# Two graph-attention layers: the fourth bank of each burst of scores is the held bank of the output products

## The chip, the cores and the metric

The kernel runs on one core of one Trainium2 chip. The metric is the device time of one execution in microseconds (us); of several executions the median is taken. Everything is computed in fp32.

## What is computed

64 examples of 256 nodes with 512 features pass through two layers with a residual each. The first is a graph attention with one head of 256 features, the second an attention with 8 heads of 64. Both are masked by one 256 x 256 adjacency. Cut to what matters here, the second layer is:

```
h = relu(layernorm(x))
q, k, v = heads(h @ Wq.T + bq), heads(h @ Wk.T + bk), heads(h @ Wv.T + bv)   # 8 heads of 64
scores = einsum('bhqd,bhkd->bhqk', q, k) / 8
scores = where(adj == 0, -inf, scores)
out = einsum('bhqk,bhkd->bhqd', softmax(scores), v)
x = x + out @ Wo.T + bo
```

## The kernel before

**Tiling and stages.** The examples go in 32 groups (g) of two (b = 0 and 1). All matmuls of the main part go through one helper (L136 and L137, so they all stand under L137), which ties each to the one before it: TensorE's order is exactly the program's order. On the other engines many operations are tied to the one before in the same way (`not_sooner`, L123, whose operations stand under L35), and a scheduler that works from its own estimate of times places the rest. The projections and the output products are done as seven half-size products each, whose operands are sums (`sums`, `o_sums`), which is why two or three accumulators are open for several products.

**The order of the work.** For each g and b a string (L1174 to L1184) is worked off letter by letter. Before it comes `weigh` (L1036) of the example before: 64 matmuls `pr` (values times probabilities, tiles of 128 x 32 of the array) into two banks, which VectorE multiplies by the reciprocal row sums `r` into `oT`. Then come the letters: S is a burst of scores (L933), m masks a pair of heads, u is one of the 21 projection products of the next group (`pq`, `pk`, `pv`), s a piece of the first layer of the group after that (`ph`, `po`, with its softmax numerator `e`), n a piece of its layer norm, f a step of the row sums (`fold`, L982: SyncE writes the probabilities to DRAM and reads them back as `parts`, POOL adds, VectorE transposes and sums them into `compact`), and o one of the seven output products of the example before (`outputs`, L1080, `py`). For b = 0, S is followed by u in the first places of TensorE's work, for b = 1 by u and s; in the last group it is followed by o. VectorE's addition of an output product into x is `x<-py,x`.

**A burst of scores.** Eight heads come as four pairs. The two heads of a pair use the upper and the lower 64 rows of the array, so their matmuls run side by side, and each head has one bank. ACT takes one exponential per head (`p<-sc`), in the order of the heads. In the traces each fp32 matmul stands as two records, so a burst has 32.

**Banks.** PSUM tiles come from four tags of one pool. `turn` has five banks that rotate; the scheduler gives a new tile the bank that it takes to come free first. Three more tags have one bank each:

```
    def mm(name):
        return psum.tile([P, 512], F32, tag="turn", name=name, bufs=5)

    def held_bank(n, name):
        return psum.tile([P, 512], F32, tag=f"held{n}", name=name, bufs=1)
```

Banks 0 and 1 of these hold the two long accumulators of the projections (L903, L914). Bank 2 holds the first accumulator of the output products (L1095), which takes four of the seven products with an addition into x after each; the other two accumulators of `outputs` (L1099, L1106), the two banks of `pr` (L1060) and all scores come from `turn`. Between the last addition of one example's `outputs` and the first product of the next one's, in which time `weigh` and the burst lie, bank 2 is empty.

Of the kernel before, what the change touches and what calls it, by code (L numbers as in the profile page):

```python
# [57 lines left out]
def bounded(  # L58
# [31 lines left out]
    NT = N // P  # L90
# [18 lines left out]
# [6 lines that stand above are left out]
    def after(instruction, name):  # L115

        tc.add_manual_dep(
            instruction.ins, name,
            mybir.DependencyInfo(mybir.DependencyClass.NoSync, mybir.DependencyReason.DATA),
            reason="the engine's order",  # L120
        )
# [14 lines left out]
    def matmul(*args, **kwargs):  # L136
        in_order(nc.tensor.matmul(*args, **kwargs))  # L137
# [795 lines left out]
    def scores(g, b):  # L933

        (q, q_tag), (k, k_tag) = (qkv[name, g, b] for name in "qk")
        name = f"{g}_{b}"
        p = att.tile([P, NQ * QH, NT, N], F32, tag="p", name=f"p_{name}", bufs=1)
        for i in range(HP):  # L940
            sc = [mm(f"sc_{name}_{2 * i + j}").rearrange("p (k n) -> p k n", k=NT) for j in range(2)]
            for kb in range(NT):
                for j in range(2):
                    rows = slice(j * DH, (j + 1) * DH)
                    matmul(
                        sc[j][:, kb, :], k[rows, i, kb * P : (kb + 1) * P], q[rows, i, :],
                        start=True, stop=True,
                    )
            pair = p[:, 2 * i : 2 * i + 2]
            for j in range(2):  # L950
                last = scalar.last
                made = scalar.activation(pair[:, j], sc[j], AF.Exp, scale=scale)
                if g == b == 0:
                    others = [last, *put_last] if i > 1 else [last]
                else:
                    others = [last, *put_last, *norm_last, *edge_last]
                for other in others:
                    after(made, other)
        places.extend((q_tag, k_tag))
        return p  # L960
# [215 lines left out]
    for g in range(NG):  # L1176
        products = project(g + 1) if g + 1 < NG else iter(())
        pieces = first_layer(g + 2) if g + 2 < NG else iter(())
        for b, parts in enumerate(steps):
# [10 lines left out]
            i, count = -1, sum(part not in "frv" for part in parts)  # L1190
            for part in parts:
                i += part not in "frv"
                if part == "u":
                    next(products, None)
                elif part == "o":
                    next(late, None)
                elif part == "s":
                    next(pieces, None)
                elif part == "n":
                    next(norms, None)  # L1200
                elif part == "m":
                    next(masks)
                elif part == "f":
                    next(folds, None)
                    continue
                elif part == "r":
                    next(additions, None)
                    continue
                elif part == "v":
                    if g < NG - 1:  # L1210
                        value_differences(g, b)
                    continue
                else:
                    waiting = (g, b, scores(g, b))
                    masks = mask_pairs(waiting[2], g == NG - 1)
                    folds = fold(*waiting)
# [384 lines left out]
```

## Time and profile before

| | |
|---|---|
| median of 3 runs | 2394.43 us (2394.31 to 2396.36) |
| profiled execution, its own time | 2394.69 us |
| its span | 2393.0 us |
| granted TensorE clock | 1.00 |
| matmul records | 15828 |
| scores: matmul records, busy time | 2048, 252.0 us |
| exponentials of scores on ACT | 512, mean 624 ns |

The page names for each group of instructions the line, the engine, the operation and its tiles, the shapes, the number, then busy time, the mean of one in ns, and the idle time before it with what ended it. PE is TensorE's matmuls, PEld its weight loads. The table of waits names who waited for whom, with the total in us, how often, and the longest. The timeline gives start and duration in us of neighbouring instructions of one kind taken together, counted from the span's start. Where it is asked for a short stretch, only the instructions that overlap the stretch are in the row.

### The profile page before, as it was taken

To read this page: it belongs to the slowest core of one execution; us is meant where nothing else is said; L and a number is where in the kernel's file an instruction comes from. 1 tells how busy PE (TensorE), PEld (TensorE's weight loads), DVE (VectorE), ACT (ScalarE), POOL (GpSimd) and SP (SyncE) were. 2 spreads that over 40 slices of the span, in tenths; PEclk is the share of its full clock that TensorE was granted. 3 is DMA by queue.
4 is the path that set the end of the run, shared out by engine and by line. 5 is a ranking of instruction groups with operands and counts; after the bars stand their busy time and mean duration, and the time that the engine had idled before them with its cause. 6 is when DMAs were issued, how large, how long until landed. Compare 5 with 4: busy or idle time off the path is not lost.

```text
span 2393.0 us, 43082 instructions
## 1 busy us (share of the span) xinstructions
PE 2381.7 (100%) x15828; PEld 2010.1 (84%) x15828; DVE 1691.4 (71%) x3345; ACT 1021.8 (43%) x2017; POOL 1422.4 (59%) x1290
## 2 busy tenths in 40 slices
PE   9999999999999999999999999999999999999998
PEld 8888888888888888888888888888888888888886
DVE  7578676676766776766777667777667676677665
ACT  5444444343444444444444434444444444344331
POOL 4565665656656655666556565556665565656552
PEclk9999999999999999999999999999999999999999
DMA  5344444544445544454444455444544444554331
GB/s 186 129 144 146 144 136 158 150 154 148 135 144 157 159 146 137 137 163 144 148 149 141 144 155 168 143 136 138 158 150 147 142 140 155 150 162 143 109 103 45
DMA packets 271865, 343.50 MB, mean 144 GB/s; under 512 B 25376, under 2 KB 217120, under 8 KB 271648
## 3 DMA queue, kind: packets, MB, share of 16 engines
q1 hardware_dynamic: 271648, 340.69, 45.6%
q8 instruction: 126, 2.06, 0.4%
q14 instruction: 91, 0.75, 0.1%
HBM read 176.95 MB, written 163.64 MB: 142 GB/s over the span
## 4 chain that ended last, share of the span: by engine, by line
PE 98%; DMA 1%; DVE 0%; ACT 0%; issue 0%; POOL 0%; SPq 0%; ACTq 0%; POOLq 0%; DVEq 0%
PE pq L137 16%; PE pv L137 16%; PE pk L137 16%; PE py L137 16%; PE sc L137 10%; PE pr L137 9%; PE ph L137 8%; PE po L137 5%; DMA adj_i<-in_adj_dram 0%; DMA wv_sb<-in_L_gnn_Wv_dram 0%; PE total L137 0%; PE gram_q L137 0%; PE gram_k L137 0%; ACT hT L35 0%; DMA parts<-rows 0%
## 5 line engine op out<-in xcount | busy, mean ns | idle before, releaser
L35 POOL TENSOR_TENSOR p<-p 128x512 f32<-128x512 f32 x248 | 383.9, 1560 | 484.9 <-DVE p L35 465.4
L35 ACT ACTIVATE xn<-x,factor 128x512 f32<-128x512 f32 x256 | 194.7, 807 | 327.3 <-POOL factor L35 319.7
L35 DVE TENSOR_TENSOR p<-p,maskT 128x1024 f32<-128x1024 f32 x254 | 328.4, 1313 | 3.2 <-ACT p L35 3.2
L35 DVE TENSOR_TENSOR x<-py,x 128x256 f32<-128x256 f32 x448 | 186.0, 416 | 188.8 <-PE py L137 182.7
L35 ACT ACTIVATE p<-sc 128x512 f32<-128x512 f32 x512 | 257.8, 624 | 141.2 <-PE sc L137 124.5
L35 POOL TENSOR_TENSOR parts<-parts 128x512 f32<-128x512 f32 x248 | 248.5, 1002 | 80.1 <-DMA parts<-rows 53.9
L137 PE MATMUL py<-wo_sb,oT 128*128 128x256 f32 x1024 | 262.4, 379 | 0.6 <-DVE oT L35 0.6
L137 PE MATMUL sc<-q,k 64*128 64x256 f32 x2048 | 252.0, 390 | 0.5 <-ACT p L35 0.5
L137 PEld LDWEIGHTS sc<-q,k 64*128 64x128 f32 x2048 | 204.5, 186 | 48.5 <-issue 26.3
L137 PE MATMUL pk<-hT,wk_sb 128*128 128x256 f32 x1024 | 244.8, 382 | 0.0
L137 PE MATMUL pq<-hT,wq_sb 128*128 128x256 f32 x1024 | 240.1, 382 | 1.1 <-ACT hT L35 0.7
L137 PE MATMUL pv<-wv_sb,hT 128*128 128x256 f32 x1024 | 236.8, 379 | 0.0
L137 PE MATMUL pr<-p,v 128*32 128x256 f32 x4096 | 234.2, 380 | 0.0
L137 PEld LDWEIGHTS pq<-hT,wq_sb 128*128 128x128 f32 x1024 | 191.8, 190 | 36.7 <-issue 10.3
L137 PEld LDWEIGHTS py<-wo_sb,oT 128*128 128x128 f32 x1024 | 194.2, 190 | 28.2 <-DVE oT L35 1.1
L137 PEld LDWEIGHTS pk<-hT,wk_sb 128*128 128x128 f32 x1024 | 189.7, 190 | 33.3 <-issue 9.9
L137 PEld LDWEIGHTS pv<-wv_sb,hT 128*128 128x128 f32 x1024 | 194.6, 190 | 26.5
L35 POOL TENSOR_TENSOR factor<-factor,rexp 128x2 f32<-128x2 f32 (+1 forms) x132 | 117.9, 893 | 161.9 <-DVE factor L35 161.4
L137 PEld LDWEIGHTS pr<-p,v 128*32 128x32 f32 x4096 | 126.8, 110 | 97.8 <-issue 15.6
L137 PE MATMUL py<-wo_sb,o_sums 128*128 128x256 f32 x768 | 197.6, 380 | 0.5 <-DVE x L35 0.5
L137 PE MATMUL pk<-sums,wk_sb 128*128 128x256 f32 x768 | 181.5, 379 | 0.0
L137 PE MATMUL pv<-wv_sb,sums 128*128 128x256 f32 x768 | 181.4, 379 | 0.0
(150 smaller groups left out, 4073.0 us busy)
## 6 DMA issues: line engine op xcount, KB each, us to landing
passed<-xt SPq DMA_DIRECT2D x124, 512.0 KB, 3.1
moved<-passed SPq DMA_DIRECT2D x496, 128.0 KB, 3.4
rows<-p SPq DMA_DIRECT2D x124, 512.0 KB, 3.4
parts<-rows SPq DMA_DIRECT2D x496, 128.0 KB, 2.9
x<-in_x_dram SPq DMA_DIRECT2D x64, 512.0 KB, 4.4
out_dram<-x SPq DMA_DIRECT2D x62, 512.0 KB, 4.0
own<-line SPq DMA_DIRECT2D x30, 256.0 KB, 3.1
wq_sb<-in_L_gnn_Wq_dram SPq DMA_DIRECT2D x2, 512.0 KB, 9.4
```

Of the source, the lines that this page charges most:

```text
L35: instruction = getattr(self.engine, operation)(*args, **kwargs)
L137: in_order(nc.tensor.matmul(*args, **kwargs))
```

## The change

The fourth score of each burst (its name ends in `_3`) no longer takes a bank of the five that rotate but the held bank 2. The other seven scores take rotating banks as before.

```
         for i in range(HP):
-            sc = [mm(f"sc_{name}_{2 * i + j}").rearrange("p (k n) -> p k n", k=NT) for j in range(2)]
+            sc = [f"sc_{name}_{2 * i + j}" for j in range(2)]
+            sc = [held_bank(2, at) if at.endswith("_3") else mm(at) for at in sc]
+            sc = [bank.rearrange("p (k n) -> p k n", k=NT) for bank in sc]
             for kb in range(NT):
                 for j in range(2):
                     rows = slice(j * DH, (j + 1) * DH)
```

The instructions of TensorE, ACT and POOL stand in the same order in both built programs. On VectorE and SyncE the scheduler moves some: in the b = 0 step, VectorE's transpose and sum of the first quad of row sums go behind nine instructions of the first layer, and at its end, just before the b = 1 burst, the last addition into x goes ahead of the transpose and sum of the second quad; in the b = 1 step two transposes of the second layer's norm go ahead of an addition and a statistic, and SyncE issues one of the four `parts` transfers of the second quad seven transfers later.

## The prediction

> **What bounds the kernel now.** I read the page's first two parts first, then the PE groups of part 5, then the table of waits for PE's weight loads, and last the timeline of two bursts of scores.
>
> ```profile
> PE 2381.7 (100%) x15828; PEld 2010.1 (84%) x15828; DVE 1691.4 (71%) x3345; ACT 1021.8 (43%) x2017; POOL 1422.4 (59%) x1290
> PE 98%; DMA 1%; DVE 0%; ACT 0%; issue 0%; POOL 0%; SPq 0%; ACTq 0%; POOLq 0%; DVEq 0%
> L137 PE MATMUL sc<-q,k 64*128 64x256 f32 x2048 | 252.0, 390 | 0.5 <-ACT p L35 0.5
> ```
>
> TensorE is the bound for the whole span, and it hardly ever shows as idle: 0.5 us before the scores in 2393. But the ends of matmuls are modelled and overlap, so a wait of 0.1 us between two of them leaves no idle time there. The row of weight loads shows some of it:
>
> ```profile
> PEld sc L137 <- issue: 26.3, 64, 0.4
> PEld pr L137 <- issue: 15.6, 47, 0.3
> ...
> PEld sc L137 <- ACT p L35: 7.7, 32, 0.9
> ```
>
> 32 times, once in half of the 64 bursts, a weight load for scores waited for an exponential (ACT, p). So the step times have to be taken from the timeline. The unit is the plain step: in the line of pk below, eight matmuls start evenly in 1.89 us and the last one is shown as 0.38, so a step is (1.89 - 0.38) / 7 = 0.216 us.
>
> ```profile
> 1067.97 1.89 PE L137 MATMUL pk<-sums,wk_sb 128*128 128x256 f32 x8
> ...
> 1074.24 3.92 PE L137 MATMUL sc<-q,k 64*128 64x256 f32 x32
> 1078.09 1.13 PE L137 MATMUL pk<-hT,wk_sb 128*128 128x256 f32 x4
> ...
> 1075.41 0.60 ACT L35 ACTIVATE p<-sc 128x512 f32<-128x512 f32 x1 [1.63 <-PE sc L137]
> 1075.41 1.09 ACT L35 ACTIVATE p<-sc 128x512 f32<-128x512 f32 x2 [1.63 <-PE sc L137]
> 1075.90 1.08 ACT L35 ACTIVATE p<-sc 128x512 f32<-128x512 f32 x2
> ...
> 1076.06 0.19 PEld L137 LDWEIGHTS sc<-q,k 64*128 64x128 f32 x2 [0.22 <-ACT p L35]
> 1076.07 0.69 PE L137 MATMUL sc<-q,k 64*128 64x256 f32 x4
> 1077.03 0.71 PE L137 MATMUL sc<-q,k 64*128 64x256 f32 x4
> 1074.24 0.70 PE L137 MATMUL sc<-q,k 64*128 64x256 f32 x4
> ```
>
> This is the burst of a group's second example. It has 32 records in two streams side by side (the two row halves of the array), so 16 steps, 16 x 0.216 = 3.46 us. It takes 1078.09 - 1074.24 = 3.85. The 0.39 over splits up as follows. Four records, two steps side by side, should show 0.38 + 0.22 + 0.01 (the skew of the streams) = 0.60. The first four show 0.70: 0.10 on entry. The four from 1076.07 show 0.69: 0.09. The four from 1077.03 show 0.71: 0.11. The remainder, 0.09, is at the exit, before pk. The two in the middle have a cause that can be read off: the first exponential ends at 1075.41 + 0.60 = 1076.01, and 0.05 later, at 1076.06, a weight load starts; the third ends at 1075.90 + 1.08 = 1076.98, and matmuls at 1077.03 are late. The bursts of the first example take the same 3.85 (1037.02 to 1040.87) with the same two stops. So each burst loses 0.20 us to exponentials that free a bank of scores.
>
> **What the Trainium skill says.** "PSUM — Partial Sum Buffer", Specifications (TRN2), gives 8 banks of 512 fp32 values. Five rotating and three held banks are all eight, which is why a score bank must wait for an earlier one's exponential. "TensorE: Matmul & The Clock Gate", Step-by-step: what each phase is for, says that TensorE pulls the next weight load ahead of matmuls in flight. The trace agrees: a load of 0.19 us costs nothing in a plain step of 0.216, so it must start one step ahead; a load let go at 1076.06 has its matmul about 0.1 later. "TensorEngine Tiling (Array Packing)", Key Properties, says that a change of tiling mode drains TensorE. The 0.10 on entry (from 128x32 tiles) and 0.09 at the exit (to 128x128) fit this, so I keep them.
>
> **The change, part by part.** No instruction is added or taken away on any engine, and TensorE's order stays. What moves is which bank a tile gets, hence which wait stands where. I number a burst's scores 0 to 7.
>
> *First example of a group (g,0).* Before, scores 3 and 4 take the banks of the two pr products, 5, 6 and 7 those of scores 0, 1 and 2, so 5 waits for the first exponential and 7 for the third; those are the two stops. After, 3 takes the held bank, 4 and 5 those of pr, 6 and 7 those of scores 0 and 1. Times within a burst, from the lines above: score 7's matmul is due at 0.10 + 12 x 0.216 = 2.70, its load one step before, 2.48. The second exponential ends at 1075.41 + 1.09 - 1074.24 = 2.26, and with 0.05 the load may go at 2.31: 0.17 to spare. Score 6 needs only the first one, 1.77. Both stops go: 0.20 a burst.
>
> *Second example (g,1).* Here the built program of before gives score 4 the bank of score 0, since the scheduler takes pr's banks to come free later. That stays in the changed program: 4 still waits for the first exponential, and the 0.09 stays. Score 6 waits for the second exponential, before and after, without loss. Score 7, however, gets the second pr bank instead of score 2's: its multiplication (oT) ends at 1075.12 by the trace, and the load is due near 1076.8. The later stop goes: 0.11 a burst.
>
> *The added waits.* Score 3 now waits for VectorE's last addition from the held bank. It ended at 1071.18, and the load is due about 1074.24 + 0.10 + 3 x 0.216 = 1074.99: 3.8 us to spare, and behind it stand all of TensorE's instructions. In the other bursts it ended 4.8 us before the burst. The next first accumulator waits for score 3's exponential; it follows several products later, and in the last group directly after the burst, where that exponential ends about 3.3 us after the start and the load is due at 3.65. So 0.
>
> *What the scheduler moves.* On VectorE, just before a (g,1) burst, the last addition into x now stands before the last transpose and sum of the row sums (0.43 and 0.42), which used to fill its wait (0.71 idle). The reciprocal, e's two operations, r and oT slip by about 0.5 us. Cover: ACT stood idle for 1.63 before the first exponential, oT is needed 1.2 later than it would come, and e's masked product (ends 1077.91) is needed by po at about 1079.7. Cost 0. Elsewhere in VectorE's order the row-sum pair of the first quad moves behind nine instructions, and two transposes (0.65 each) pass an addition; SyncE moves one of four row-sum transfers behind seven others. Their users come microseconds later by the timeline: 0, and at worst 0.1 a group (3 us), which I keep for the range.
>
> *The sum.* 29 bursts (g,0) from group 2 to 30 x 0.195 = 5.7; 29 bursts (g,1) from group 1 to 29 x 0.107 = 3.1; the very first burst 0.2. The second burst of the run lasts 4.83, because score 3 waited for the exponential of score 0, which started 1.41 in; after, its last limit is oT at 2.26 for score 5, then two plain pairs: about 4.18, so 0.65. The third lasts 4.31, with score 7 behind an exponential that starts late (1.64): 0.5. The last three last 3.90 and have no such wait for score 4: 3 x 0.24 = 0.7. Together 10.8 us. The profiled execution took 2394.69 (span 2393.0 and 1.7 around it), so 2383.9; the median of the runs shown, 2394.43, lies 0.26 below it: 2383.7.
>
> **The rivals.** *The stop moves on instead of going.* In (g,0) the margin for score 7 is 0.17; if loads need more notice than the 0.05 and one step I read, a stop of 0.11 comes back in 29 bursts: 3.1 less, 2386.8. For it: the margin is under one step. Against: before, score 6's load came with 0.2 to spare and lost nothing. *Both stops go in (g,1) too*, if the 0.09 there has another cause than the first exponential: 29 x 0.09 = 2.6 more, 2381.1. Against it stands the load at 1076.06, 0.05 after that exponential's end. *Nothing comes of it*: TensorE, early by 0.3 a group, meets another producer. The table of waits names one 0.6 us for POOL and one 0.6 for oT in the whole run, and the timeline shows kept_q and kept_k bound by their own product, so I see none: 2394. *Slower:* the row-sum chain of VectorE in (g,1). Past a slip of 1.63 us, instead of 0.5, ACT's exponentials of e run into those of the scores, and score 4, which still waits for the first, holds TensorE. At a slip of 2.3 each of 29 bursts loses 0.67, 19.4 in all, less the 10.8: 2402.3. It decides against the change from a slip of 2.0.
>
> **How the numbers follow.** The forecast 0.80, the stop that moves on 0.07, both stops gone 0.04, nothing 0.04, slower 0.05. What a measurement can tell from no change is 0.2%, 4.8 us, so faster means under 2389.6: 0.91; the same 0.04; slower 0.05. The forecast's own range is 2382 to 2386, from 3 us lost to the moved transfers or 2 us of scatter; it reaches down to both stops gone and up to the moved stop with some scatter: 2381.0 to 2387.5.
>
> **What would show it.** Right: bursts (g,0) of 3.65 and (g,1) of 3.74; no weight load of scores 5 or 7 right after an exponential in (g,0); still a load of scores waiting for ACT in (g,1), as now in 29 to 32 bursts. Wrong: a burst near 3.85; a load for scores that waits for VectorE; new idle time before po or pr; or ACT's first exponential of a (g,1) burst later than 1.17 after its start.

## The result and the profile after

| | before | after |
|---|---|---|
| median | 2394.37 us (4 runs, 2394.15 to 2396.36) | 2426.84 us (4 runs, 2426.15 to 2427.43) |
| span of the profiled execution | 2393.0 us | 2425.8 us |
| burst of scores, first example (g,0), groups 2 to 29 | 3.85 us | 3.65 us |
| burst of scores, second example (g,1), groups 2 to 29 | 3.85 us | 4.95 us (3.74 to 5.81) |

The changed kernel is slower by 32.5 us: ratio 1.0134, 95% interval 1.0116 to 1.0151. The forecast was 2383.7.

The page of the kernel after, its engine line, the shares of the chain that ended last, and the two rows of scores (busy time and mean, then idle time before and what ended it):

```profile
PE 2391.4 (99%) x15828; PEld 2005.6 (83%) x15828; DVE 1712.9 (71%) x3345; ACT 1020.1 (42%) x2017; POOL 1431.3 (59%) x1290
...
PE 87%; DMA 4%; DVE 3%; ACT 3%; issue 2%; POOL 1%; SPq 0%; ACTq 0%; DVEq 0%; POOLq 0%
...
L137 PE MATMUL sc<-q,k 64*128 64x256 f32 x2048 | 255.1, 386 | 22.0 <-ACT p L35 22.0
L137 PEld LDWEIGHTS sc<-q,k 64*128 64x128 f32 x2048 | 201.3, 186 | 76.4 <-ACT p L35 34.2
```

Engine shares hardly move. The chain does: TensorE carried 98% of it before and carries 87% now. A tenth of it leads through DMA, VectorE, ACT and POOL, so now and then a chain outside TensorE comes later than TensorE. Where it enters is in the idle column: before the scores TensorE stood 0.5 us before and stands 22.0 us now, for ACT's exponentials.

The table of waits of the kernel after, weight loads only (total, times, longest):

```profile
PEld sc L137 <- ACT p L35: 34.2, 32, 2.0
...
PEld pv L137 <- ACT kept_v L35: 11.8, 28, 1.6
```

As before, 32 loads of scores wait, but up to 2.0 us where it was 0.9. The second line is new: the first products of v wait for ACT's copies.

So the first examples behave as forecast, and the second examples lose more than they could gain. The timelines of two second examples show what is late, first in the kernel before (the burst starts at 1074.24), then in the kernel after (at 1015.44). Columns are start, duration, engine, line, operation; SPq is the issue of a transfer by SyncE.

```profile
1060.73 0.43 DVE L35 STREAM_TRANSPOSE parts<-parts 128x256 f32<-128x256 f32 x1
1061.20 0.42 DVE L35 TENSOR_REDUCE compact<-parts 128x8 f32<-128x256 f32 x1
1061.53 0.42 DVE L35 TENSOR_TENSOR H<-ph,kept_h 128x258 f32<-128x258 f32 x1
...
1069.17 0.43 DVE L35 STREAM_TRANSPOSE parts<-parts 128x256 f32<-128x256 f32 x1
1069.63 0.42 DVE L35 TENSOR_REDUCE compact<-parts 128x8 f32<-128x256 f32 x1
...
1073.83 1.29 DVE L35 TENSOR_TENSOR oT<-pr,r 128x512 f32<-128x512 f32 x2
...
1061.69 2.79 SPq L35 DMA_DIRECT2D parts<-rows  x4
1064.53 0.53 SPq L35 DMA_DIRECT2D line<-rows  x1
1067.05 0.34 SPq L35 DMA_DIRECT2D own<-line  x1
...
1070.68 1.70 ACT L35 ACTIVATE e<-own,H 128x256 f32<-128x256 f32 x4
```

```profile
1002.40 0.43 DVE L35 TENSOR_TENSOR H<-ph,kept_h 128x258 f32<-128x258 f32 x1 [0.40 <-PE ph L137]
...
1005.23 0.43 DVE L35 STREAM_TRANSPOSE parts<-parts 128x256 f32<-128x256 f32 x1
1005.70 0.42 DVE L35 TENSOR_REDUCE compact<-parts 128x8 f32<-128x256 f32 x1
...
1012.79 0.45 DVE L35 STREAM_TRANSPOSE parts<-parts 128x256 f32<-128x256 f32 x1 [0.41 <-POOL parts L35]
1013.27 0.42 DVE L35 TENSOR_REDUCE compact<-parts 128x8 f32<-128x256 f32 x1
...
1017.67 1.29 DVE L35 TENSOR_TENSOR oT<-pr,r 128x512 f32<-128x512 f32 x2
...
1006.19 1.73 SPq L35 DMA_DIRECT2D parts<-rows  x4
1007.96 0.53 SPq L35 DMA_DIRECT2D line<-rows  x1
1010.70 0.34 SPq L35 DMA_DIRECT2D own<-line  x1
...
1014.51 1.71 ACT L35 ACTIVATE e<-own,H 128x256 f32<-128x256 f32 x4 [2.52 <-DMA passed<-xt]
...
1017.51 4.00 ACT L35 ACTIVATE p<-sc 128x512 f32<-128x512 f32 x8
...
1015.44 2.00 PE L137 MATMUL sc<-q,k 64*128 64x256 f32 x16
1018.15 2.26 PE L137 MATMUL sc<-q,k 64*128 64x256 f32 x16 [0.71 <-ACT p L35]
```

Count every start from its burst's start. VectorE's pair for the first quad of row sums (transpose, sum into `compact`) stands at -13.51 before and at -10.21 after: 3.30 later, since eight instructions of the first layer and of the next norm (from the second addition into `H` to `factor`) now go ahead of it. SyncE issues the four transfers of the second quad, `parts<-rows`, 0.07 us after that pair's end in both kernels (1061.20 + 0.42 to 1061.69; 1005.70 + 0.42 to 1006.19), so they are 3.30 later too. Two tables of SyncE's own waits name the sum of such a pair, in the kernel before

```profile
SPq L35 <- DVE compact L35: 227.0, 60, 7.7
```

and in the kernel after:

```profile
SPq L35 <- DVE compact L35: 241.6, 32, 10.8
```

From the fetch the lateness goes down two ways and comes together again: the second quad's pair is 2.42 later, ACT's first operation of `e` 2.63 (-3.56 to -0.93), and `oT` 2.64 (-0.41 to 2.23). ACT's first exponential of the scores comes at 2.07 in place of 1.17. Of the two ways the own scores end last. By the trace's landing times `own` lands at 1014.18 in this burst, 0.34 ahead of `e`, while the second quad's sum ends at 1013.69, 0.82 ahead. In groups 2 to 28 the distances are 0.10 to 0.34 and 0.45 to 1.12. The transfer named in the bracket, `passed<-xt`, lands only after `e` has started, so it isn't the cause.

The last two lines show what that does to TensorE. Half of the burst, eight steps, is through at about 1.83; scores 4 and 5 then wait, score 4 for the first exponential, score 5 for the first half of `oT`. Matmuls start again at 2.71 in the one stream (the exponential ended 0.05 before), and in the other at 2.98 (0.05 after that half). In the mean over groups 2 to 29 the first exponential starts at 2.13, the first `oT` ends at 2.97, and the burst lasts 4.95.

Over all 64 bursts, the time beyond 16 steps of 0.216 us is 26.8 us before and 51.4 after: 24.6 of the 32.5 us lie in the bursts. The rest, 7.9 us, lies mostly later in the same groups, where the weight loads of pv wait.

### The profile page after: what moved, and what is told of

Same layout as the page of the kernel before. It is cut to its first block, busy times and chain, and to the rows that moved or that the text cites. A ratio compares the mean times of both kernels' runs of the same rounds, so it can differ in the third digit from the quotient of the medians.

```text
span 2425.8 us, 43056 instructions
## 1 busy us (share of the span) xinstructions
PE 2391.4 (99%) x15828; PEld 2005.6 (83%) x15828; DVE 1712.9 (71%) x3345; ACT 1020.1 (42%) x2017; POOL 1431.3 (59%) x1290
## 4 chain that ended last, share of the span: by engine, by line
PE 87%; DMA 4%; DVE 3%; ACT 3%; issue 2%; POOL 1%; SPq 0%; ACTq 0%; DVEq 0%; POOLq 0%
PE pq L137 16%; PE pv L137 16%; PE py L137 14%; PE pk L137 14%; PE sc L137 8%; PE ph L137 8%; PE pr L137 6%; PE po L137 4%; ACT e L35 2%; DMA passed<-xt 1%; DMA own<-line 1%; DVE e L35 1%; DVE p L35 1%; ACT p L35 1%; DMA line<-rows 0%
## 5 line engine op out<-in xcount | busy, mean ns | idle before, releaser
L35 POOL TENSOR_TENSOR p<-p 128x512 f32<-128x512 f32 x248 | 392.9, 1598 | 453.6 <-DVE p L35 451.0
L35 DVE TENSOR_TENSOR p<-p,maskT 128x1024 f32<-128x1024 f32 x254 | 347.5, 1389 | 3.2 <-ACT p L35 3.2
L137 PE MATMUL pq<-sums,wq_sb 128*128 128x256 f32 x768 | 181.5, 379 | 0.0
```

What stands on the lines that cost most here:

```text
L35: instruction = getattr(self.engine, operation)(*args, **kwargs)
```

## The experiments

Each kernel was timed beside the kernel before on the same chip. The edits are against the changed kernel.

**Is it the order or the bank?** The theory at this point, T1: on VectorE the first quad's pair is late; SyncE's fetch waits for the buffer that the pair frees; the second quad's sums and, behind the fetch in SyncE's queue, the row of own scores (`line`, `own`, the input of `e`) come late. Its rivals: R1, the last addition into x ahead of the second quad's pair, the slip that the forecast counted as covered; R2, the bank; R3, SyncE's one moved transfer.

*One tie that undoes R1's part.* `after` ties an instruction behind another in its engine's order; `fold_last` is the last sum of the row sums so far.

```
-            vector.tensor_add(to, out, to)
+            return vector.tensor_add(to, out, to)
...
         product(first, 3, False)
-        add(0, 1, first)
+        last = add(0, 1, first)
+        if b == 1:
+            for other in fold_last:
+                after(last, other)
```

> The changed kernel with one tie: in the second examples the last addition into x stands behind the second quad's row-sum pair, as before the change; the first quad's pair stays late. T1 (the first quad's pair does it): 2420 to 2428, bursts (g,1) still near 5 us, with 0.5 us less at most. Rival R1 (the last addition, which the forecast counted as a slip of 0.5 us): about 2384, bursts (g,1) 3.74.

Measured: 2425.78 us, bursts (g,1) 4.96. R1 falls: the last addition isn't what makes the bursts long. What it costs by itself this run can't tell, since the pair is late in it too.

*The bank in one of the two examples only.*

```
-            sc = [held_bank(2, at) if at.endswith("_3") else mm(at) for at in sc]
+            sc = [held_bank(2, at) if b == 0 and at.endswith("_3") else mm(at) for at in sc]
```

> Score 3 on the held bank only in the first example of a group; the second examples use the turning banks as before. The first quad's pair is late as in the changed kernel. T1: bursts (g,1) still late, and worse than in the changed kernel, since with four turning banks score 3 waits for the first exponential and score 4 for oT0: 5.2 to 5.6 us, time 2430 to 2442. Rival R2 (the bank in the second examples does the harm): bursts (g,1) 3.85 as before, time about 2389 (-5.8 of the first examples alone).

Measured: 2437.87 us; bursts (g,0) 3.65, (g,1) 5.62. And with `b == 1` in place of `b == 0`:

> Score 3 on the held bank only in the second example of a group. VectorE's and SyncE's order stays that of the kernel before (but for one swap in the first group). T1: bursts (g,1) 3.74, bursts (g,0) 3.85, time about 2391 (-3.2). Rival R2: bursts (g,1) near 5 us, time 2415 to 2430.

Measured: 2390.50 us (ratio 0.9984, interval 0.9978 to 0.9991); bursts (g,0) 3.85, (g,1) 3.74. The bank in the second examples is harmless and even brings its 0.11 us. The loss in the second examples comes with the bank in the *first* examples, and without a held bank of their own they lose more (5.62 against 4.95). R2 falls. The link between the two is the order: VectorE's order is that of the changed kernel wherever the first examples use the held bank, and that of the kernel before where they don't.

*The order put back, first attempt.* The addition that makes part of `H` tied behind the pair, and all the additions into x of second examples tied to the program's order.

```
-        vector.tensor_add(part(1, 0), second, p16)
+        made = vector.tensor_add(part(1, 0), second, p16)
+        for other in fold_last:
+            after(made, other)
...
         def add(t, half, out):
             to = xt[:, t, half * D // 2 : (half + 1) * D // 2]
-            vector.tensor_add(to, out, to)
+            last = vector.last
+            made = vector.tensor_add(to, out, to)
+            if b == 1:
+                after(made, last)
```

> The changed kernel with VectorE's order in the second examples put back by ties: the first quad's row-sum pair (32x32 transpose and reduce) ahead of the addition that makes H, and output products' additions held to the program's order, so that the last of them follows the second quad's pair again. The bank of score 3 is the changed kernel's, and SyncE's order with its one moved transfer too. Theory T1 (the pair, 3.3 us late, holds the one buffer, so SyncE's fetch of the second quad and the row of own scores behind it come 2.5 us late and ACT's exponentials of the second example's scores with them): bursts (g,1) fall from 4.97 to about 3.74 us, (g,0) stay 3.65, time about 2384 (-10.8 against before). Rival R2 (the bank itself, or score 3's wait on it): about 2426 as in the changed kernel. Rival R3 (SyncE's moved transfer): about 2426, since that stays moved.

Measured: 2418.65 us, far from the 2384 that T1 gave. But the trace says that the cause was gone and the ties had brought others: ACT's first exponential of (g,1) is back at 1.16, yet the table of waits of this kernel's weight loads has

```profile
PEld py L137 <- DVE x L35: 25.9, 32, 0.9
...
PEld sc L137 <- ACT p L35: 12.6, 60, 0.5
```

where the kernel before has 1.7 in 4 waits and 7.7 in 32. The additions, held in program order, keep output products waiting for their bank. And a burst (g,1), 4.22 long, has a second stop at an exponential: in group 10 the second one ends 2.25 us after the burst's start, and the load of a score that waits for ACT starts at 2.30. `oT` also comes 0.43 us later (its first half ends at 0.72 in place of 0.29), but that is 1.1 us before the second half of the burst begins, so it doesn't explain the stop. An undo that moves other instructions too proves little.

*The order put back, second attempt.* Five ties (the text below counts six): the one in `H`, three single additions into x (each behind the one instruction that it followed before), and one addition of k. VectorE's order around the second examples is then that of the kernel before, instruction for instruction; the bank and SyncE's moved transfer stay.

```
         product(second, 7, True)
-        add(1, 1, second)
+        last = vector.last
+        made = add(1, 1, second)
+        if b == 1:
+            after(made, last)
...
         product(second, 4, False)
-        add(1, 0, second)
+        made = add(1, 0, second)
+        if b == 1:
+            for other in turn_last:
+                after(made, other)
```

> The changed kernel with six ties that put VectorE's order around the second examples' row sums back to that of the kernel before, instruction for instruction: the first quad's pair stands between the two additions into H again, the second quad's pair ahead of the last addition into x. Bank use and SyncE's one moved transfer stay as in the changed kernel. The earlier attempt at this held the additions into x to the program's order and so made TensorE wait 0.8 us a group for one of them and oT come 0.43 us later; here no such wait is expected. T1: bursts (g,0) 3.65, (g,1) 3.74 us, weight loads for scores no longer wait 2.0 us, time 2382 to 2387. Rivals R2 (bank) and R3 (SyncE's moved transfer): 2420 to 2428.

Measured: 2384.56 us (ratio 0.9961, interval 0.9947 to 0.9974). Bursts (g,0) 3.654, (g,1) 3.742. In this kernel's page TensorE's idle time before scores is gone:

```profile
L137 PE MATMUL sc<-q,k 64*128 64x256 f32 x2048 | 242.2, 385 | 0.1
```

R2 and R3 are out: same bank, same moved transfer, 42.3 us less than the changed kernel. That is the 32.5 us lost and the 9.8 that the change was to gain. The order on VectorE is the whole loss.

**What does the late pair hold up?** A pair late by 3.3 us should cost nothing by itself: in the kernel before its result is first read 9.5 us after its end (1061.62, and `compact`'s reciprocal at 1071.10). T1 in its sharper form blamed SyncE's queue: the own scores stand behind a fetch that waits. "DMA: Bandwidth & Descriptors" in the Trainium skill, Anatomy of one DMA (its path from GpSimd), says that the transfer engines do not wait on semaphores; the wait is made by the issuing sequencer. Here SyncE issues, and the timelines above agree: `line<-rows` is issued 0.04 to 0.05 us after the four fetches ahead of it end, in both kernels, though `rows` was written well before in the kernel after (at about 1003). So in this run the own scores went first, with VectorE's order unchanged. The letters are those of the first examples' string; f is a step of the row sums.

```
-    steps = ("Smmnfuuuumonmnuofuusssosfsfssuvnofunonfosuo",
+    steps = ("Smmnfuuuumonmnuofuusssosfsssuvnfofunonfosuo",
```

> The changed kernel, VectorE's order left as it is, the first quad's pair late; only SyncE's queue differs: the two transfers of the own scores stand ahead of the four that fetch the second quad's rows in the first examples. T1 in its sharper form (the late pair holds the one buffer, the fetch waits for it at the head of SyncE's queue, and the own scores behind it are what comes too late): the own scores are issued near 5 us earlier, e is ready 1 to 2 us earlier than in the changed kernel, oT0 ends near 1.5 us after the burst's start instead of 2.9, bursts (g,1) 3.74 us and time 2383 to 2390. Rival T1b (the second quad's own sums are what is late, whoever stands behind them in the queue): bursts stay near 5 us, time 2415 to 2428.

Measured: 2420.83 us, a seventh of the loss back; bursts (g,1) 4.74. The sharper form falls: the own scores do come last in the changed kernel, but with them out of the way something else holds `e` almost as long. The timeline says what (burst at 1238.68):

```profile
1228.95 0.42 DVE L35 TENSOR_REDUCE compact<-parts 128x8 f32<-128x256 f32 x1
...
1236.12 0.45 DVE L35 STREAM_TRANSPOSE parts<-parts 128x256 f32<-128x256 f32 x1 [0.50 <-POOL parts L35]
1236.60 0.42 DVE L35 TENSOR_REDUCE compact<-parts 128x8 f32<-128x256 f32 x1
...
1228.11 0.35 SPq L35 DMA_DIRECT2D own<-line  x1
1229.44 1.74 SPq L35 DMA_DIRECT2D parts<-rows  x4
...
1237.10 1.71 ACT L35 ACTIVATE e<-own,H 128x256 f32<-128x256 f32 x4 [1.87 <-issue]
```

The own scores are issued at 1228.11, nine microseconds ahead, and `e` still starts only at 1237.10: 0.08 us after the second quad's sum ends (1236.60 + 0.42). It does not read that sum. It takes its buffer: `fold` asks for `parts` of first examples under the tag `e` with one buffer, the same that `first_layer` asks for `e`. The buffer goes from the first quad's sums to the second quad's and then to `e`, and each owner waits for the last reader of the one ahead.

```
        pool, tag, bufs = (att, "e", 1) if b == 0 else (big, "hT0", 2)
...
        both = att.tile([P, GB, NT, N], F32, tag="e", name=f"e_{g}", bufs=1)
```

Moving the f by a single place instead (`sosfssfsuvno` for `sosfsfssuvno`) has the pair 1.14 us later than before, but the fetch behind the own scores:

> The changed kernel with one letter of the schedule of first examples moved one place: the first quad's sum and the fetch of the second quad come after the last products of H instead of before. VectorE then has the pair 1.2 us later than in the kernel before instead of 3.3, and SyncE the own scores ahead of the fetch. T1: no late exponentials, bursts (g,1) 3.74, time 2382 to 2387. T1b: a gain in part, since the pair is still 1.2 us late: 2395 to 2405.

Measured: 2423.79 us, bursts (g,1) 4.84. Both theories missed: the fetch is issued at -9.93, 2.62 us later than in the kernel before, since `own` ahead of it in the queue has to wait for `line` to land. In both of these kernels `e` starts 0.08 us after the second quad's sum in the burst shown, so it hangs on the fetch into the one buffer. In the changed kernel the own scores, behind that fetch in the queue, come later still.

Theory T2 is that chain of one buffer. It has a direct test: take the second quad out of it, and leave everything else, the late pair included, as the change made it. The tag `moved` has two buffers of the same size that are free at that time.

```
-            parts = pool.tile([P, P // S, N], F32, tag=tag, name=f"parts_{g}_{b}_{quad}", bufs=bufs)
+            own, n = ("moved", 2) if b == 0 and quad == 1 else (tag, bufs)
+            parts = pool.tile([P, P // S, N], F32, tag=own, name=f"parts_{g}_{b}_{quad}", bufs=n)
```

> The changed kernel with one more edit: in the first examples the second quad's partial sums are fetched into a free buffer of another tag (moved) instead of the one that the first quad's partial sums leave and that e takes afterwards. The order of instructions on every engine and on SyncE is that of the changed kernel (but for two swaps at the ends); the first quad's pair stays 3.3 us late on VectorE. T2, formed after the own scores put first gave only a seventh of the loss back (one buffer goes from the first quad's sums to the second quad's and then to e, so the late pair holds up all three in a row): SyncE's fetch no longer waits for the pair, own scores and second quad's sums come on time, e is written when own lands, bursts (g,1) 3.74 us, time 2382 to 2390. Rival (a pair late on VectorE costs by itself, whatever buffer is behind it): bursts stay near 5 us, time 2415 to 2428.

Measured: 2384.61 us (ratio 0.9960, interval 0.9946 to 0.9974), bursts 3.654 and 3.742. The row of SyncE's waits for `compact` that is shown above is gone from this kernel's table. Its timeline (burst at 1216.20):

```profile
1206.01 0.43 DVE L35 STREAM_TRANSPOSE parts<-parts 128x256 f32<-128x256 f32 x1
...
1199.44 1.73 SPq L35 DMA_DIRECT2D parts<-rows  x4
...
1205.70 0.34 SPq L35 DMA_DIRECT2D own<-line  x1
...
1212.65 1.70 ACT L35 ACTIVATE e<-own,H 128x256 f32<-128x256 f32 x4
...
1216.11 1.29 DVE L35 TENSOR_TENSOR oT<-pr,r 128x512 f32<-128x512 f32 x2
```

The pair is as late as in the changed kernel (-10.19). The fetch goes 6.6 us ahead of it, `e` starts at -3.55 as in the kernel before, and the loss is gone. From the timeline of one burst of each kernel, in us from its start (the last two columns are the mean and the time):

| kernel | pair of quad 0 | fetch of quad 1 | `e` on ACT | mean (g,1) burst | time |
|---|---|---|---|---|---|
| before | -13.51 | -12.55 | -3.56 | 3.85 | 2394.4 |
| order put back | -13.51 | -12.55 | -3.56 | 3.74 | 2384.6 |
| second buffer | -10.19 | -16.76 | -3.55 | 3.74 | 2384.6 |
| f one place later | -12.37 | -9.93 | -1.37 | 4.84 | 2423.8 |
| own scores first | -10.20 | -9.24 | -1.58 | 4.74 | 2420.8 |
| after | -10.21 | -9.25 | -0.93 | 4.95 | 2426.8 |

**Can the second examples do as well as the first?** With the order put back, score 4 still stops 0.09 us for the first exponential. Here a second held bank, the one that the projection of k has free, takes score 3, and bank 2 takes score 4:

```
-            sc = [held_bank(2, at) if at.endswith("_3") else mm(at) for at in sc]
+            held = {f"sc_{name}_3": 2}
+            if b == 1 and 0 < g < NG - 1:
+                held = {f"sc_{name}_3": 1 - turn[0], f"sc_{name}_4": 2}
+            sc = [held_bank(held[at], at) if at in held else mm(at) for at in sc]
```

> The order put back by six ties, and in the second examples scores 3 and 4 on held banks: 3 on the one that the running projection of k has free, 4 on the one of the output products, so that score 5 waits for what oT1 or the first exponential frees and none waits for oT0 within the burst. T1: bursts (g,1) 3.65 as the first examples', 0.09 less than with one held bank, 29 times: time 2380 to 2384, 2 to 3 us under the order put back alone. If the bank of the projection is not free in time: 2385 to 2400.

Measured: 2384.26 us, bursts (g,1) 3.735. No gain: score 5 now waits for the first exponential in place of score 4, and the two run side by side, so the stop stays (0.08).

## Why the prediction was wrong

*Right: what bounds the kernel, and both halves of the gain.* With the order put back the bursts last 3.654 and 3.742 us; 3.65 and 3.74 were forecast. The sum of 10.8 us stands against 9.8 measured (2394.39 to 2384.56), the forecast of 2383.7 against 2384.56. One term of the sum was off: the third burst of the run, to be 0.5 shorter than its 4.31, lasts 4.45. That score 4 keeps its stop in (g,1) while the later stop goes was right too; the bank in the second examples alone gives 4.0, where 3.1 was counted for groups 1 to 29 and some more for the ends of the run.

*Right: score 3's wait on the held bank costs nothing.* With the bank and the order apart, there is no loss.

*Nearly right: the last addition into x.* Its slip was counted as 0.5 us under a cover of 1.63. It stays moved in the kernel with the second buffer, where `oT` starts 0.32 us later in the burst than before (-0.09 in place of -0.41) and the time is 2384.61: no cost shows.

*Wrong: one step.* "Elsewhere in VectorE's order the row-sum pair of the first quad moves behind nine instructions, and two transposes (0.65 each) pass an addition; SyncE moves one of four row-sum transfers behind seven others. Their users come microseconds later by the timeline: 0, and at worst 0.1 a group (3 us)". (The timeline shows eight instructions, not nine.) The transposes and SyncE's transfer were indeed free: they stay moved in kernels of 2384.6. The row-sum pair, put at 0 to 0.1 us a group, costs 42.3 us, about 1.4 a group. A sign that the prediction itself had named came with it: the first exponential, due 1.17 us after a burst's start, comes at 2.13 in the mean. The step looked for the users of the pair's *result*, `compact`, which is read at -3.1 (the reciprocal at 1071.10). It did not ask who takes the pair's *buffer*: the second quad's fetch does, and `e` then waits for what stands behind that fetch, the own scores and the same buffer. The trace of the kernel before has a hint of it: the four transfers stand 0.07 us after the end of the pair, from which they read nothing, and SyncE's waits name its sum.

*The slower rival had the right cover and the wrong source.* It said that past a slip of 1.63 us ACT's exponentials of `e` run into those of the scores. The slip measured is 2.63, which leaves 1.00; the first exponential comes 0.90 later in the burst shown and 0.97 in the mean. But the prediction counted the slip from the last addition alone, 0.5, and gave the rival a chance of 0.05. The rival also made score 4's exponential the only brake. At a slip of 2.63 that gives 1.00 us a burst (its 0.67 is for a slip of 2.3); measured are 1.20 above the 3.74 that the burst has with the order put back, since `oT`, late by 2.64, holds score 5 beyond score 4. Its time of 2402.3 is also 0.7 short of its own terms (2394.4 + 19.4 - 10.8 = 2403.0).

*The sum by what was measured.* Against the order put back, the changed kernel has 51.4 - 16.6 = 34.8 us more in its bursts, of 42.3. The other 7.5 go, as far as the tables show, with the new wait of pv for `kept_v`. That wait is in each kernel that has a late `e` and the held bank in both examples (11.4 to 11.8 us in the table of waits, with 6.8 to 8.1 us that the bursts don't explain), and it is gone where `e` is on time (0.2 and 0.4). In the kernel with the bank in first examples only it is 1.8, and there the bursts explain the whole difference. ACT's copies stand there behind normalisations that wait for POOL. That these are late because of the same slip is a reading of the tables, not shown.

Left open: how late `e` would be if it alone had another buffer and the fetch still waited. Since the own scores land last in the changed kernel, it should gain nothing; this was not tried. The two ways were separated only by sending the own scores first. Why the scheduler moves the pair when the first examples take the held bank was not looked into.

## What to carry to other kernels

When a scheduler moves an instruction, ask three questions: who reads its result, who overwrites its operands, and what stands behind those two on their queues. Here the second question had the nearest answer: a transfer issued 0.07 us after an instruction from which it reads nothing was waiting for its buffer. Such a short distance is a reason to look, not a proof; the proof was the second buffer. And look at orders before the arithmetic: here a change of banks in one example's burst changed the order of another engine, and one buffer of another tag gave back 42.2 us where the change itself gives 9.8.

## What was not expected of the hardware

The chain of transfers looks quiet here only as long as it is hidden. In the kernels where `e` is on time, all 28 bursts (g,1) of groups 2 to 29 last the same to 2 ns (3.849 to 3.851 before, 3.741 to 3.742 with the order put back). In the kernel after, whose groups also repeat one order of instructions, the fetch and `e` are on the path, and they scatter between 4.59 and 5.81 us in groups 2 to 28. With the own scores first it is 4.10 to 5.56, and one of 8.11. The transfers of row sums take 2.4 to 4.8 us from issue to landing in the kernel after, median 3.0, and 2.4 to 5.4 in the kernel before; `line` and `own` take 2.5 to 3.9 after and 2.4 to 3.7 before. The scatter is there in both; only its cover differs.
